# The heads of a graph attention layer: the denominators divided out ahead of Wo, and Wo as 64x64 quarters

## The chip, the cores and the metric

The kernel runs on one core of a Trainium2 chip. A core has five engines that run side by side, each with its own queue in order: TensorE for matrix products (PE in the profile, and PEld for its weight loads), VectorE (DVE), ScalarE (ACT), GpSimd (POOL) and SyncE (SP), which here only issues transfers. 16 DMA engines move data between DRAM and SBUF, the memory on the chip; TensorE writes into PSUM. The metric is the time of one execution on the device in microseconds, as the median of several runs.

## The reference, cut to what matters

Four graph layers run one after the other, each as `x = layernorm(x + layer(x))`, on x of 8 batches, 2048 nodes and 64 features. The change is in the last, a graph attention with 4 heads, followed by a second attention over the product with Wo:

```
h = einsum('bnc,hdc->bhnd', x, Wh)
out_h = gat(h) + bh           # softmax over the neighbours of h.h, times h
cat = out_h as [b, n, 4*64]
z = leaky_relu(cat, 0.2)
h2 = einsum('bnk,dk->bnd', z, Wo)
out2 = gat(h2) + bo
out = layernorm(leaky_relu(out2, 0.2)) * gamma + beta
```

Inside `gat` the sums over the neighbours are divided by the sum of the weights, the denominator, one for each batch, head and node. leaky_relu(a / s) is leaky_relu(a) / s where s is positive, and Wo is linear within a head; so the division may stand at any place from the sums to the sum over heads.

## The kernel before

The graph is sparse. The nodes are handled as 16 tiles of 128 (`NT`), each as 2 groups of 64 nodes (`NG`), each group with 5 sections of 128 gathered neighbours (`GS`): 160 steps for the heads, 10 per tile. A step k consists of these pieces, in a program order that is written out by hand for PE, ACT, DVE and POOL (`manual_schedule`; SP's transfers are issued as the code comes to them):

- `fetch(k + 7)`: POOL gathers 128 rows of 2 KB from the table xtab into xs (L203), 12 buffers
- `turn(k + 2)`: four PE transposes of xs (L1038), copied out by ACT (L1040)
- the work `beside`, one entry for each step of a tile (j = 0 to 9)
- `score(k + 1)`: scores into PSUM (pscore, two buffers, L1051), exponentials on ACT (L1054), times the edges on DVE (L1057)
- `back(k - 1)`: the sums over neighbours on PE (po, L1073). Twice for each group a block of 32 nodes is complete, and DVE copies it to `o` (L1080). xs carries a column of ones, so one row of `o` for each half of the partitions holds the denominators. After the last block of a tile (at j=0 of the next tile) SP writes these two rows to DRAM (dtab, L1084) and reads them back as 32 rows of 128 nodes (dT, L1086).

`beside` before, for the tile ahead (+1) and the tile just summed (-1): j=0 turn_nodes (+1), j=1 sides (+1, heads 0 and 1), j=2 and j=3 through_w (-1), j=4 sides (+1, heads 2 and 3) with `sums` (-1) ahead of it, j=5 to j=8 through_wo (-1, one head each), j=9 pieces (-1).

`through_w` brings two heads of `o` through the weights and leaky_relu into z: its products are `quarters` (L1014), 64x64 blocks of the 128x128 array, then a copy on ACT (L1103) and DVE's leaky product (L1104). z has features on partitions and nodes along the row. `sums` turns dT on PE (L1092) and DVE inverts into recs (L1095, L1097): nodes on partitions. `wo_products` (L1110) multiplies a head's z, four 128x128 blocks, by a block-diagonal Wo into PSUM with nodes on partitions (pm, one buffer); `add_head` multiplies by the inverses on DVE (L1116) and adds the heads up on POOL (L1120). At the last head POOL adds bo (L1124) and SP writes ktab (L1125). `pieces` splits h2 into three bf16 parts on ACT, DVE and POOL (L1138 to L1141), writes them to ptab (L1142), and POOL adds a bias to X (L1143).

The last tile is done after the loop, with add_head on DVE. Then the second attention (`fifth`) gathers from ktab for all tiles. At its end all inverses are checked against bounds (L1383 to L1385); the flag decides whether a slow path runs.

Of the kernel before, what the change touches and what calls it, by code (L numbers as in the profile page):

```python
# [21 lines left out]
F32 = mybir.dt.float32  # L22
# [26 lines left out]
def kernel(ctx: ExitStack, tc: tile.TileContext, ins: dict, out: bass.AP):  # L49
# [622 lines left out]
    f3w = fast.enter_context(tc.tile_pool(name="f3w", bufs=1))  # L672
    recs = f3w.tile([P, NT, HN + 1, B], F32, name="recs")
    early = ExitStack()
# [317 lines left out]
    ktab = dram.tile([N, BD], F32, name="ktab")  # L992
    dtab = dram.tile([NT, 2 * HN * NP, P], F32, name="dtab")
    bo = rows("bo", ins["L3_gnn_bo"], f3w)
    b3 = rows("b3", ins["L3_gnn_beta"], f3w)
    with early, ExitStack() as heads:
# [5 lines left out]
        ps_m = heads.enter_context(tc.tile_pool(name="f3psm", bufs=1, space=PSUM))  # L1002
        Us, os, xss, xsTs, ws, pos, h2s, zs, dTs = ({} for _ in range(9))

# [54 lines left out]
        def back(k):  # L1059
            it, g, s = steps[k]  # L1060
            xs, w = xss.pop(k), ws.pop(k)

            for blk, a, b in blocks_of(s):
                if s == OPEN[blk]:
                    pos[it, g, blk] = ps_o.tile([P, NP, HN, GB], F32, name="po")
                po = pos[it, g, blk]
                for p in range(NP):
                    for k_ in range(2):  # L1070
                        half = slice(k_ * D, (k_ + 1) * D)
                        f0 = p * P + k_ * D
                        nc.tensor.matmul(po[half, p, :, a - blk * GB:b - blk * GB], xs[:, f0:f0 + D],  # L1073
                                         w[:, k_, p, :, a - WINDOWS[s][0]:b - WINDOWS[s][0]],
                                         start=(s == OPEN[blk] and p == 0), stop=(s == CLOSE[blk] and p == NP - 1))
            for blk, a, b in blocks_of(s):
                if s == CLOSE[blk]:
                    if (g, blk) == (0, 0):
                        os[it] = wk.tile([P, HN, NP, P], F32, name="o")
                    nc.vector.tensor_copy(os[it][:, :, :, node_block(g, blk)].rearrange("p h a i -> p a h i"), pos.pop((it, g, blk)))  # L1080
            if (g, s) == (NG - 1, TURN[-1]):
                rows_of = dtab[it].rearrange("(k n) i -> k (n i)", k=2)
                for k_ in range(2):
                    nc.sync.dma_start(rows_of[k_:k_ + 1], os[it][k_ * D:k_ * D + 1].rearrange("p h a i -> p (h a i)"))  # L1084
                dTs[it] = wk.tile([2 * HN * NP, P], F32, name="dT")
                nc.sync.dma_start(dTs[it], dtab[it])  # L1086


        def sums(it, pool=None):
            dT = dTs.pop(it)  # L1090
            pd = pool.tile([P, 2 * HN * NP], F32, name="pt") if pool else misc([P, 2 * HN * NP])
            nc.tensor.transpose(pd, dT, ident[0:2 * HN * NP, 0:2 * HN * NP])  # L1092
            pd = pd.rearrange("p (k h a) -> p h a k", k=2, h=HN)
            rec = recs[:, it, 0:HN].rearrange("p h (a k) -> p h a k", k=2)
            nc.vector.reciprocal(rec[:, :, 0:2], pd[:, :, 0:2])  # L1095
# [3 lines left out]
        def through_w(it, h0):  # L1099
# [4 lines left out]
            nc.vector.scalar_tensor_tensor(z.rearrange(flat), z.rearrange(flat), 0.2, z.rearrange(flat), op0=ALU.mult, op1=ALU.max)  # L1104

        def wo_products(it, h, pool=None):
            z = zs[it, h - h % 2]
# [5 lines left out]
        def add_head(it, h, ph):  # L1113
            eng = nc.vector if it == NT - 1 else nc.gpsimd
            dst = wk.tile([P, B, D], F32, name="h2h" if h else "h2")
            nc.vector.tensor_tensor(dst, ph.rearrange("p a (k d) -> p (a k) d", k=2), along(recs[:, it, h]), ALU.mult)  # L1116
            if h == 0:
                h2s[it] = dst
            else:
                eng.tensor_tensor(h2s[it], h2s[it], dst, ALU.add)  # L1120
            if h == HN - 1:
                h2f = h2s[it].rearrange("p b d -> p (b d)")
                hb = wk.tile([P, B, D], F32, name="hb")
                eng.tensor_tensor(hb, h2s[it], over(bo, hb.shape), ALU.add)  # L1124
                nc.sync.dma_start(ktab[it * P:(it + 1) * P, :], hb.rearrange("p b d -> p (b d)"))  # L1125
                if it == 0:
                    sq = wk.tile([P, BD], F32, name="h2h")
                    nc.scalar.activation(sq, h2f, AF.Square, accum_out=shift)

        def through_wo(it, h):  # L1130
            add_head(it, h, wo_products(it, h))

        def pieces(it):

            h2f = h2s[it].rearrange("p b d -> p (b d)")
            hp3 = wk.tile([P, 3, BD], BF16, name="hp3")
            rest = wk.tile([P, BD], F32, name="rest")
            nc.scalar.copy(hp3[:, 0], h2f)  # L1138
# [6 lines left out]
        def node_side(it, pool, **kw):  # L1145
# [13 lines left out]
        beside = {  # L1159
            0: (turn_nodes, 1), 1: (sides, 1, 0), 2: (through_w, -1, 0), 3: (through_w, -1, 2), 4: (sides, 1, 2),  # L1160
            5: (through_wo, -1, 0), 6: (through_wo, -1, 1), 7: (through_wo, -1, 2), 8: (through_wo, -1, 3), 9: (pieces, -1),
        }
# [4 lines left out]
        with tc.manual_schedule(engines=engines):  # L1167
# [7 lines left out]
            for k in range(len(steps) + 1):  # L1175
# [4 lines left out]
                it, j = divmod(k, PER)  # L1180
                if j == 4 and 0 < it < NT:
                    sums(it - 1)
                f, t, *a = beside[j]
                if k < len(steps) and 0 <= it + t < NT:
                    f(it + t, *a)
                if k + 1 < len(steps):
# [8 lines left out]
            ph = wo_products(t, 0)  # L1195
            sums(t, ps_t)
            add_head(t, 0, ph)
# [4 lines left out]
    with ExitStack() as fifth:  # L1202
# [75 lines left out]
        def invert(it):  # L1278
            nc.vector.reciprocal(recs[:, it, HN], sums[it][1])

        def divide(it):
            po, rd = sums[it][0], recs[:, it, HN]
            z = zs[it] = fk.tile([P, B, D], F32, name="z", bufs=6)
# [95 lines left out]

        nbad = fp.tile([P, 8], F32, name="nbad")  # L1380
        chk = fp.tile([P, NT * (HN + 1) * B], BF16, name="chk")
        recf = recs.rearrange("p t h b -> p (t h b)")
        nc.vector.tensor_scalar(chk, recf, 2.0**-115, None, op0=ALU.is_ge)  # L1383
        nc.vector.scalar_tensor_tensor(chk, recf, 2.0**60, chk, op0=ALU.is_le, op1=ALU.mult, accum_out=nbad[:, 0:1])
        nc.vector.tensor_scalar(nbad[:, 0:1], nbad[:, 0:1], float(NT * (HN + 1) * B), None, op0=ALU.not_equal)  # L1385
        lack = fp.tile([P, 5, NT], F32, name="lack")
# [12 lines left out]
        nc.vector.tensor_scalar(nbad[:, 6:8], bounds[:, 0:2], S_MAX, 1.0, op0=ALU.is_le, op1=ALU.not_equal)  # L1399
        pb = ps_d.tile([1, 8], F32, name="pd")  # L1400
        nc.tensor.matmul(pb, ones_col, nbad, start=True, stop=True)
        sb = fp.tile([1, 1], F32, name="sb")
        nc.vector.tensor_reduce(sb, pb, AX.X, ALU.add)
        nc.vector.tensor_copy(flag, sb)
        bad = nc.values_load(flag[0:1, 0:1], min_val=0, max_val=P * (3 + 5 * NT))
    fast.close()
# [543 lines left out]
```

## Time and profile before

| | us |
|---|---|
| median of 3 runs | 1881.07 (1874.75 to 1881.57) |
| the profiled execution: its time | 1880.07 |
| its span, first to last instruction | 1878.2 |
| PE busy in the span | 1363.0 (73%) |
| DVE busy | 1336.7 (71%) |
| ACT busy | 978.5 (52%) |
| POOL busy | 965.1 (51%) |
| heads stage, first L1038 to the last step | 955 to 1480 |
| L1110, products with Wo: 512 instructions, median of one | 0.275 |
| L1116, DVE, times the inverses: 64, median of one | 0.69 |
| L1120, POOL, sum of the heads: 45 | 1.276 |

The times of the engines overlap, so their sum means nothing; a share of the whole span is an average over stages with different limits, and the one that matters here is that of the heads stage. A product of float32 shows in the profile as two matmul instructions, a transpose as one; the durations of matmuls overlap in the array, so the cost of a group is read from where the next one starts.

### The profile page before, as it was taken

The page shows a single profiled execution, that of the slowest core. Times are in us where ns is not written, and L with a number is a line of the kernel's source. Part 1 is how long each engine was busy: PE and PEld are TensorE (multiplying, and loading weights), DVE is VectorE, ACT ScalarE, POOL GpSimd, SP SyncE. Part 2 cuts the span into 40 slices and gives each one's busy share as a digit, 9 for nine tenths or more (in the row PEclk, how much of TensorE's full clock was granted, in tenths as well). Part 3 has the DMA queues.
Part 4 walks back from the last instruction along what each step waited for, and adds up shares of the span by engine and source line. Part 5 has one row for each costly group of instructions (what it writes and reads, how often), then busy time and mean ns, then how long its engine had stood idle before and what let it go on. Part 6 is the DMA issues. An engine that isn't in the chain of part 4 may idle for free.

```text
span 1878.2 us, 33889 instructions
## 1 busy us (share of the span) xinstructions
PE 1363.0 (73%) x12656; PEld 835.2 (44%) x12656; DVE 1336.7 (71%) x2975; ACT 978.5 (52%) x2405; POOL 965.1 (51%) x889
## 2 busy tenths in 40 slices
PE   3663346551789996997669999999999665566653
PEld 3563223330333334522258888888888521111110
DVE  6879579896676546666735666666666589889887
ACT  4643235545942225355645555555555257677675
POOL 0000376670664543675345565655656388666651
PEclk9955567766799998999779999999999878767776
DMA  7422476660237971365342333332423265455441
GB/s 205 135 90 90 121 203 192 191 202 13 99 113 282 318 265 56 124 194 155 101 118 89 95 110 105 96 119 84 123 87 112 74 191 171 132 154 153 139 111 25
DMA packets 125660, 255.26 MB, mean 136 GB/s; under 512 B 62480, under 2 KB 65040, under 8 KB 123408
## 3 DMA queue, kind: packets, MB, share of 16 engines
q0 software_dynamic: 56320, 188.78, 33.3%
q1 hardware_dynamic: 52528, 60.03, 9.6%
q10 hardware_dynamic: 16640, 4.20, 1.0%
q8 instruction: 102, 1.67, 0.4%
q14 instruction: 70, 0.57, 0.1%
HBM read 217.04 MB, written 35.91 MB: 135 GB/s over the span
## 4 chain that ended last, share of the span: by engine, by line
PE 39%; DVE 12%; ACT 11%; issue 5%; POOL 3%; DMA 1%; ACTq 0%; SPq 0%; POOLq 0%; DVEq 0%
PE pscore L1051 9%; PE po L1073 6%; PE pa L588 5%; PE pt L1038 5%; PE pscore L1014 3%; PE pm L1110 3%; ACT z L169 3%; PE pa L643 2%; ACT wx L1256 2%; DVE sc L1245 2%; PE py L789 2%; DVE pr L1240 1%; DVE st L155 1%; POOL hs L203 1%; PE pa L959 1%
## 5 line engine op out<-in xcount | busy, mean ns | idle before, releaser
L203 POOL DMA_INDIRECT hs<-htab,src x160 | 153.2, 957 | 265.9 <-ACT selTf L431 206.6
L1057 DVE SCALAR_TENSOR_TENSOR w<-w,Sel 128x640 f32<-128x640 f32 (+2 forms) x160 | 170.7, 1073 | 128.2 <-ACT w L1054 128.2
L203 POOL DMA_INDIRECT xs<-xtab,src x160 | 191.6, 1197 | 55.3 <-issue 25.7
L588 PE MATMUL pa<-R,ET 128*128 128x512 bf16 x768 | 182.2, 395 | 49.1 <-POOL R L576 35.7
L203 POOL DMA_INDIRECT hs<-ktab,src x160 | 159.1, 995 | 45.5 <-issue 36.2
L1051 PE MATMUL pscore<-U,xsT 64*128 64x80 f32 (+2 forms) x2560 | 182.1, 282 | 0.0
L1051 PEld LDWEIGHTS pscore<-U,xsT 64*128 64x128 f32 x2560 | 156.9, 189 | 37.2 <-ACT xsT L1040 22.7
L1054 ACT ACTIVATE w<-pscore 128x640 f32<-128x640 f32 (+2 forms) x160 | 119.6, 748 | 99.9 <-PE pscore L1051 98.8
L169 ACT ACTIVATE X<-X,ln_m,ln_r 128x64 f32<-128x64 f32 x256 | 87.2, 428 | 138.9 <-DVE ln_m L161 138.9
L588 PEld LDWEIGHTS <-ET 128*128 128x128 fp8e4 x768 | 75.4, 101 | 163.8 <-issue 85.4
L1040 ACT COPY xsT<-pt 128x512 f32<-128x512 f32 x160 | 93.7, 586 | 100.5 <-PE pt L1038 99.5
L1235 PE MATMUL pe<-hi,selTb 64*128 64x512 bf16 x480 | 89.0, 489 | 74.7 <-DVE pr L1240 69.0
L1120 POOL TENSOR_TENSOR h<-h,h2h 128x512 f32<-128x512 f32 x45 | 57.4, 1276 | 161.7 <-DVE h2h L1116 161.7
L1073 PE MATMUL po<-w,xs 128*64 128x88 f32 (+2 forms) x3072 | 138.7, 236 | 1.1 <-DVE w L1057 1.1
L1038 PE MATMUL pt<-ident,xs 128*128 128x128 f32 x640 | 106.3, 289 | 25.0 <-DMA xs<-xtab,src 23.9
L1073 PEld LDWEIGHTS po<-w,xs 128*64 128x64 f32 x3072 | 113.4, 137 | 15.0 <-DVE w L1057 1.4
L203 POOL DMA_INDIRECT rs<-rtab,src x80 | 75.9, 949 | 62.4 <-PE pa L643 43.0
L1240 DVE TENSOR_TENSOR pr<-pe,hs 128x1024 f32<-128x1024 f32 x80 | 97.3, 1216 | 14.6 <-DMA hs<-ktab,src 10.7
L1256 ACT ACTIVATE wx<-hs,w 128x64 f32<-128x64 f32 x424 | 106.7, 344 | 0.0
L597 DVE RECIPROCAL rec<-pa 128x256 f32<-128x256 f32 x32 | 54.1, 1730 | 64.1 <-PE pa L643 38.0
L1245 DVE TENSOR_REDUCE sc<-pr 128x16 f32<-128x1024 f32 x80 | 97.1, 1214 | 2.0
L460 DVE TENSOR_TENSOR hs<-hs,w 128x1024 f32<-128x1024 f32 x80 | 91.8, 1212 | 3.2 <-ACT w L449 3.2
(628 smaller groups left out, 3188.4 us busy)
## 6 DMA issues: line engine op xcount, KB each, us to landing
at<-in_adj SPq DMA_DIRECT2D x16, 1024.0 KB
rtab<-r SPq DMA_DIRECT2D x16, 512.0 KB
ptab<-hp SPq DMA_DIRECT2D x16, 384.0 KB
hi<-ptab SPq DMA_DIRECT2D x16, 384.0 KB
X<-in_x ACTq DMA_DIRECT2D x16, 256.0 KB
htab<-H SPq DMA_DIRECT2D x16, 256.0 KB
ytab<-y SPq DMA_DIRECT2D x16, 256.0 KB
ktab<-hb SPq DMA_DIRECT2D x16, 256.0 KB
```

The source lines that it names most:

```text
L169: nc.scalar.activation(v[:, b], v[:, b], AF.Identity, scale=rstd[:, k:k + 1], bias=nmr[:, k:k + 1])
L203: nc.gpsimd.indirect_dma_start(out=dst, out_offset=None, in_=table[:, :], in_offset=bass.IndirectOffsetOnAxis(ap=src[:, it, s, g:g + 1], a ...
L588: nc.tensor.matmul(po[h].rearrange("p a f -> p (a f)"), ET[:, jt, it * P:(it + 1) * P], R[:, jt, q, h].rearrange("p a f -> p (a f)"), star ...
L1038: nc.tensor.transpose(pt[:, p], xss[k][:, p * P:(p + 1) * P], ident)
L1040: nc.scalar.copy(xsTs[k], pt)
L1051: nc.tensor.matmul(pscore[:, k_, f0:f0 + HN * ni].rearrange("p (h i) -> p h i", i=ni), xsT[half, p], Us[it][half, p, :, i0:i0 + ni], start ...
L1054: nc.scalar.activation(w.rearrange("p k a h i -> p k (a h i)"), pscore[:, :, 0:NP * HN * ni], AF.Exp)
L1057: nc.vector.scalar_tensor_tensor(wt, wt, 3.0e38, edge, op0=ALU.min, op1=ALU.mult)
L1073: nc.tensor.matmul(po[half, p, :, a - blk * GB:b - blk * GB], xs[:, f0:f0 + D], w[:, k_, p, :, a - WINDOWS[s][0]:b - WINDOWS[s][0]], start ...
L1240: nc.vector.tensor_tensor(pr.rearrange("p k b d -> p (k b d)"), pes[u].rearrange("p k b d -> p (k b d)"), hss[u].rearrange("p k b d -> p ( ...
L1245: nc.vector.tensor_reduce(sc, pr, AX.X, ALU.add)
L1256: nc.scalar.activation(wxs[u][:, 0, b], hss[u][:, 0, b], AF.Copy, scale=ws[u][:, 0, b:b + 1])
```

## The change

The division moves from behind Wo to ahead of it. In place of `sums` (at j=4) there is `invert` at j=3: DVE inverts dT as it lies (32 rows of 128), SP writes the inverses to a DRAM table itab and reads them back as R, broadcast over the 64 partitions of each half: four transfers with 64 x 4 runs of 256 numbers, 1 MB together. DVE also checks the bounds of the inverses here, on the 32 rows. At j=5 and j=6 `divide` multiplies z by R on POOL, two heads at a time. At j=7 `wo_all` multiplies all four heads by Wo as 64x64 quarters with 256 columns and adds the heads up in PSUM (in a pscore buffer); ACT copies the sum out as hT, features on partitions. At j=8 `turn_back` transposes hT, four times 128x128, ACT and DVE copy the result to h2, with the two halves of the partitions put back in their places, and POOL adds bo as before. DVE's products with the inverses and POOL's additions of the heads are gone, but for the last tile, which keeps the old way with `last_invert`. `o`, `h2h` and `rest` have one buffer in place of two. The checks at the end take the inverses of the second attention, those of the last tile, and the counts from `invert`.

```diff
-    recs = f3w.tile([P, NT, HN + 1, B], F32, name="recs")
+    recs = f3w.tile([P, NT, B], F32, name="recs")
+    last_recs = f3w.tile([P, HN, B], F32, name="last_recs")
+    RD = 2 * HN * NP
+    recT = f3w.tile([RD, P], F32, name="recT")
+    few = f3w.tile([RD, NT], F32, name="few")
...
-                        os[it] = wk.tile([P, HN, NP, P], F32, name="o")
+                        os[it] = wk.tile([P, HN, NP, P], F32, name="o", bufs=1)
...
-        def sums(it, pool=None):
+        def invert(it):
             dT = dTs.pop(it)
...
+            rT = wk.tile([RD, P], F32, name="rT")
+            nc.vector.reciprocal(rT, dT)
+            nc.sync.dma_start(itab[it], rT)
+            nc.vector.tensor_scalar(recT, rT, 2.0**-115, None, op0=ALU.is_ge)
+            nc.vector.scalar_tensor_tensor(recT, rT, 2.0**60, recT, op0=ALU.is_le, op1=ALU.mult, accum_out=few[:, it:it + 1])
+            R = Rs[it] = wk.tile([P, HN, 2, 2, P], F32, name="R", bufs=1)
+            rows_of = itab[it].rearrange("(k h j a) i -> k h j (a i)", k=2, h=HN, j=2)
+            for q in range(2):
+                for j in range(2):
+                    nc.sync.dma_start(R[q * D:(q + 1) * D, :, j].rearrange("p h a i -> p h (a i)"),
+                                      rows_of[q if j == 0 else 1 - q, :, j].unsqueeze(0).to_broadcast([D, HN, 2 * P]))
...
+        def divide(it, h0):
+            z = zs[it, h0].rearrange("p j h a n -> p j h (a n)")
+            nc.gpsimd.tensor_tensor(z, z, Rs[it][:, h0:h0 + 2].rearrange("p h j a n -> p j h (a n)"), ALU.mult)
+
+        def wo_all(it):
+            ph = ps_s.tile([P, 2, CW], F32, name="pscore")
+            for h in range(HN):
+                z = zs[it, h - h % 2]
+                for k in range(2):
+                    own = slice(k * D, (k + 1) * D)
+                    for j in range(2):
+                        to = own if j == 0 else slice((1 - k) * D, (2 - k) * D)
+                        nc.tensor.matmul(ph[to, j, 0:2 * P], WoT[own, h, own],
+                                         z[own, j, h % 2].rearrange("p a n -> p (a n)"), start=(h == 0), stop=(h == HN - 1))
+            hTs[it] = wk.tile([P, 2, 2, P], F32, name="hT")
+            nc.scalar.copy(hTs[it].rearrange("p j a n -> p j (a n)"), ph[:, :, 0:2 * P])
+
+        def turn_back(it):
+            hT = hTs.pop(it)
+            ph = misc([P, 2, 2, 2, D])
+            for j in range(2):
+                for a in range(2):
+                    nc.tensor.transpose(ph[:, j, a].rearrange("p k d -> p (k d)"), hT[:, j, a], ident)
+            h2s[it] = wk.tile([P, B, D], F32, name="h2")
+            h2 = h2s[it].rearrange("p (j a k) d -> p j a k d", j=2, a=2)
+            nc.scalar.copy(h2[:, 0], ph[:, 0])
+            for k in range(2):
+                nc.vector.tensor_copy(h2[:, 1, :, k], ph[:, 1, :, 1 - k])
+            with_bo(it, nc.gpsimd)
...
-            0: (turn_nodes, 1), 1: (sides, 1, 0), 2: (through_w, -1, 0), 3: (through_w, -1, 2), 4: (sides, 1, 2),
-            5: (through_wo, -1, 0), 6: (through_wo, -1, 1), 7: (through_wo, -1, 2), 8: (through_wo, -1, 3), 9: (pieces, -1),
+            0: [(turn_nodes, 1)], 1: [(sides, 1, 0)], 2: [(through_w, -1, 0)], 3: [(invert, -1), (through_w, -1, 2)],
+            4: [(sides, 1, 2)], 5: [(divide, -1, 0)], 6: [(divide, -1, 2)], 7: [(wo_all, -1)], 8: [(turn_back, -1)], 9: [(pieces, -1)],
...
-                if j == 4 and 0 < it < NT:
-                    sums(it - 1)
```

## The prediction

> **What bounds the kernel now.** I read the busy time by stage first, then the waits inside the stage that the change touches, then one tile of that stage in order of time. The heads stage runs from 955 us (first turn of a gathered tile, L1038) to 1480 us. Three rows of the table of stretches; the columns are the length, then busy time of PE, PEld, DVE, ACT, POOL, the granted clock, the DMA share and GB/s:
>
> ```profile
> 1100.00:1200.00 100.00, 100.00 (x1506) 83.31 (x1506) 64.49 (x83) 54.63 (x83) 59.62 (x48) 1.00 0.35 105
> 1200.00:1300.00 100.00, 100.00 (x1513) 83.87 (x1512) 63.76 (x83) 54.94 (x83) 59.63 (x48) 1.00 0.34 102
> 1300.00:1400.00 100.00, 100.00 (x1505) 83.92 (x1503) 63.77 (x80) 54.43 (x82) 59.65 (x48) 1.00 0.34 101
> ```
>
> PE is busy all the time at a granted clock of 1.00; DVE has a third of its time free, POOL 40%. In the waits from 1100 to 1400 us the longest is POOL's at L1120, which costs nothing; PE's queue has none over 0.4 us. So a microsecond of PE work added or removed moves the end, and so does any wait put into PE's order. The period of a tile is 32.70 us (its o copies end at 1190.48 and 1223.18). Now one tile in order of time (start, length):
>
> ```profile
> 1190.50 0.53 SPq L1084 DMA_DIRECT2D dtab<-o  x2
> 1190.72 0.66 PE L1038 MATMUL pt<-ident,xs 128*128 128x128 f32 x4
> 1191.30 0.64 PEld L1014 LDWEIGHTS pscore<-o,AT 64*64 64x64 f32 x16 [0.17 <-DVE U L1024]
> 1192.33 0.97 PEld L1051 LDWEIGHTS pscore<-U,xsT 64*128 64x128 f32 x16 [0.39 <-ACT xsT L1040]
> 1193.73 0.31 SPq L1086 DMA_DIRECT2D dT<-dtab  x1
> ...
> 1195.87 0.96 POOL L203 DMA_INDIRECT xs<-xtab,src  x1 [0.30 <-issue]
> ...
> 1201.41 0.65 PE L1038 MATMUL pt<-ident,xs 128*128 128x128 f32 x4
> 1201.80 0.97 PEld L1110 LDWEIGHTS pm<-WoT,z 128*128 128x128 f32 x8
> 1202.89 0.97 PEld L1051 LDWEIGHTS pscore<-U,xsT 64*128 64x128 f32 x16
> ...
> 1207.16 1.28 POOL L1120 TENSOR_TENSOR h<-h,h2h 128x512 f32<-128x512 f32 x1 [9.07 <-DVE h2h L1116]
> ...
> 1215.44 0.97 PEld L1051 LDWEIGHTS pscore<-U,xsT 64*128 64x128 f32 x16 [0.17 <-issue]
> ...
> 1217.20 0.66 PE L1038 MATMUL pt<-ident,xs 128*128 128x128 f32 x4
> 1217.58 0.47 PEld L699 LDWEIGHTS pm<-ident,X 128*128 128x128 f32 x4
> ...
> 1218.22 0.97 PEld L1051 LDWEIGHTS pscore<-U,xsT 64*128 64x128 f32 x16 [0.17 <-issue]
> ```
>
> The reader is to see the gap that a piece of work makes between a step's turn (pt) and its score. With one head through Wo it is 1202.89 - 1201.41 = 1.48 us; with nothing between 0.59 (in the ninth step pt starts at 1214.85, score at 1215.44); with four 128x128 transposes 1.03 (1217.19 to 1218.22); one call of quarters, eight 64x64 products of two heads, takes 1.03 (1191.30 to 1192.33) after 0.59 of approach.
>
> **The change on PE.** I write j for the step in the tile. j=4 loses the transpose of the denominators (1198.46 to 1198.63): -0.17. j=5 and j=6 lose a head each: 1.48 to 0.59, -0.89 twice. j=7 gets wo_all, sixteen 64x64 products of 256 columns, which is two calls of quarters: 0.59 + 2 x 1.03 = 2.65 for 1.48, +1.17. j=8 gets turn_back, four transposes: 1.03 for 1.48, -0.45. Sum -1.23 us per tile. The last tile keeps the old way, so 15 tiles: -18.5 us, if PE never waits.
>
> **The new chain.** Now the denominators are needed before Wo, and they get there by o copy, dtab, dT, reciprocal, itab, R, two divisions on POOL. Before, the inverses were first used at j=5 through a path that ended at j=4 on PE. I count from T, the end of the last o copy, when dtab is issued (1190.50).
>
> - dtab to dT landed. dT is issued 3.2 us after dtab here, 2.5 (1288.60 to 1291.07) to 4.2 (1027.11 to 1031.34) in others; at the last tile, where PE waits for it, dT lands 1.63 after its issue (1481.75 to 1483.38). While gathers run it is later: the packets of dT end between 4.5 and 7.0 us after T, median 5.2, plus 0.2 for the semaphore. T+5.4. DVE is free by T+5.0 (its score product of j=2 ends at 1195.47), so it stands waiting; behind it stands through_w's second leaky product, wanted only at j=7.
> - Reciprocal of 32x128. L1095 takes 244 ns for 16 columns, L597 1730 for 256: 6.2 ns a column, 0.93 us. T+6.3.
> - itab written, R issued. The pair dtab, dT gives 2.2 to 3.9 from the last write's issue to the read's issue; 2.75. T+9.1. SP has nothing else queued until ktab at j=8.
> - R: four DMAs, 64x4 rows of 1 KB each, 1 MB per tile. The trace has 128 packets of 1 KB for xtab at 929.4 to 930.1 us at about 300 GB/s: 3.5 us, after 0.9 us from issue to first packet (ktab at 1184.53 starts to move at 1185.4) and before 0.3 of completion. T+13.8. Bounds: 2.5 us at the 420 GB/s of ktab's best slices, 7.0 if the rate halves because each DMA writes 64 partitions and not 128. The nearer row has packets of the same size, so 3.5.
> - divide, 128x1024 on POOL, twice, with the gather of j=6 between them. An addition of two 128x512 takes 1276 ns; a cast goes from 724 (512) to 1323 (1024), so 125 ns are fixed and 1024 columns cost 2.4. Bounds: 1.91 (L1261, where one operand is repeated) and 2.55. Gather 1.25 and 0.3 of issue. L1057 on DVE grows from 0.82 to 2.67 us at most when POOL adds or multiplies at the same time, so the two hold each other up; I give the second divide 0.3. T + 13.8 + 2.4 + 1.55 + 0.3 + 2.4 + 0.1 = T+20.6.
>
> **Where PE needs it.** Without waits pt of j=7 would come at 1207.96 - 1.95 = 1206.01; the heads 2 and 3 of wo_all then start 0.59 + 1.03 later, at 1207.63, T+17.1. The first division is ready at T+16.2, just in time for heads 0 and 1. So PE waits 3.5 us at wo_all in each tile. Queued behind it on PE are the score and the sums of that step, on ACT the copy hT and the exponentials, so the stall goes through to T of the next tile and isn't made up. Net 3.5 - 1.23 = +2.3 us per tile, 15 tiles: +34.5 us.
>
> [...]
>
> **What lies beside.** DVE loses four products of 0.69 and three small reciprocals per tile and gets the 0.93, two checks of 32x128 (0.2 each at most, from 128x8 at 0.17 and 128x640 at 0.49) and two copies of 128x128 (0.2 to 0.3): lighter by over 1 us. POOL loses three additions (3.8 us) and gets 4.8: 24 us of a 35 us period. While it waits for R, about 7 us, no gather is issued; seven steps of gathers are ahead, over 16 us, which hides it; without that cover the 7 us would fall on PE. ACT gets hT (0.59, as L1040) and half of h2 (0.35), in gaps of 45% of its time. The score product blocked by a division (2.4) has 4 us until its sums (exponentials of 1204 feed sums at 1210). o with one buffer is next written at j=3, when its products and dtab are 3 us past. The checks at the end replace 1.44 us of DVE (L1383 to L1385) by some ten operations of 0.1 to 0.25 us in a place where DVE waits for ACT until 1861.7: nothing, 0.5 us if ACT were early. The last tile's tail from 1480 us, on the old path, is the same.
>
> **Sum.** Span 1878.2 + 34.5 = 1912.7, with the 1.9 us around it (1880.07) 1914.6; the median of the runs shown, 1881.07, lies 1.0 above the profiled time, so 1915.
>
> **Rivals.**
> 1. The chain fits. With every low bound, dT at T+4.1, reciprocal 0.9, itab 2.2, R 0.9 + 2.5 + 0.2, divisions of 1.91 and a gather of 1.25, the second division ends at T+16.0, before PE asks at T+17.1. Then the full 18.5 us are won: 1862.5. It needs my chain to be 3.5 us too long; at 2.3 too long the change is level. For it: POOL idles there and SP has nothing else to do. Against: five steps in a row at the low end. Chance 0.14, with 0.11 between this and level, near 1881.
> 2. R is the long pole: its rate halved, 7.0 us, stall 7.0, net +5.8 per tile, +87: 1968; at the midpoint of the two times +60, 1941. For it: halves of 64 partitions and one source read by 64 rows. Against: the 1 KB row. It decides from R over 5 us. Chance 0.18.
> 3. wo_all isn't two calls of quarters, because four heads add up in the same PSUM rows and each has to wait for the one ahead: twice the time, 2.06 more, of which the first half hides under the stall; +15 us on the forecast, 1930, or 1881 to 1893 if the chain fits. For it nothing in this trace; L1073 adds in PSUM without a gap. Chance 0.05.
>
> **How the numbers follow.** The forecast as it stands, 1893 to 1940, has 0.52; it is the likeliest, so 1915. With rivals 2 and 3 slower has 0.75, within 0.5% (about what a measurement of this kernel can tell from no change, 9 us) 0.11, faster 0.14. The range goes down to 1869, which takes in level and part of the gain, and up to 1955, R at about 6.2 us; the likeliest case alone is 1893 to 1940.
>
> **What will show it.** PE's idle time before the wo_all line, released by POOL's division, near 3.5 us times 15, and PE's busy share in the stage falling to about 90%; a period of 35 us; dT to R landed about 8.4 us; divisions of 2.4 us with POOL idle before the first, ended by DMA R; wo_all's products in 2.1 us. The prediction is wrong if POOL reaches the first division after R has landed, if the waits of PE name another engine, or if the tile is shorter than 32.7 us.

## The result and the profile after

The changed kernel takes 2002.21 us (median of 6 runs, 1999.36 to 2005.74); the kernel before takes 1880.51 beside it (6 runs, 1874.75 to 1881.57). The ratio is 1.065, 95% interval 1.063 to 1.067: 122 us slower, where 34 were forecast and the range reached to 74. The direction was right, the size was not. A single run more than 1.5% above the fastest of its kernel (there are two, both on a slower chip of the experiments) is left out of the times and ratios below.

First the table of stretches of the changed kernel, with the columns and the stretches that the prediction showed of before:

```profile
1100.00:1200.00 100.00, 89.57 (x1228) 71.00 (x1226) 44.42 (x61) 47.05 (x74) 48.85 (x37) 0.85 0.37 105
1200.00:1300.00 100.00, 86.87 (x1236) 67.89 (x1232) 46.92 (x64) 46.84 (x71) 46.67 (x37) 0.88 0.41 113
1300.00:1400.00 100.00, 89.23 (x1180) 70.24 (x1184) 41.44 (x58) 45.16 (x71) 49.01 (x37) 0.81 0.37 105
```

PE is idle for 11.4% of the time (265.66 of 300 busy), and, what no term of the prediction allowed for, its granted clock is 0.81 to 0.88 where it was 1.00. In the same busy time fewer products get done: 1180 to 1236 per 100 us, before 1505 to 1513. The writes to dtab come at 1197.31, 1238.11 and 1279.42: a tile takes 40.8 to 41.3 us in place of 32.70, 8.1 to 8.6 more, and 15 tiles by 8.1 are the 122 us.

Now one tile in order of time (start, length, engine, line, shape; in brackets the idle time of the engine just before, and what ended it):

```profile
1197.31 0.53 SPq L1089 DMA_DIRECT2D dtab<-o  x2
...
1200.33 0.31 SPq L1091 DMA_DIRECT2D dT<-dtab  x1
...
1202.93 0.94 DVE L1097 RECIPROCAL rT<-dT 32x128 f32<-32x128 f32 x1
...
1203.90 0.31 SPq L1098 DMA_DIRECT2D itab<-rT  x1
...
1206.58 2.92 SPq L1105 DMA_DIRECT2D R<-itab  x4
...
1211.60 1.13 PE L1056 MATMUL pscore<-U,xsT 64*128 64x88 f32 x16
...
1214.41 2.34 POOL L1127 TENSOR_TENSOR z<-z,R 128x1024 f32<-128x1024 f32 x1 [10.18 <-DMA R<-itab]
...
1216.81 1.09 PE L1137 MATMUL pscore<-z,WoT 64*64 64x256 f32 x16 [2.79 <-POOL z L1127]
1217.92 2.35 POOL L1127 TENSOR_TENSOR z<-z,R 128x1024 f32<-128x1024 f32 x1
...
1220.32 1.99 PE L1137 MATMUL pscore<-z,WoT 64*64 64x256 f32 x16 [2.41 <-POOL z L1127]
...
1222.23 2.00 PE L1056 MATMUL pscore<-U,xsT 64*128 64x80 f32 x16
```

Two things are to be seen. PE waits twice per tile, here 2.79 and 2.41 us, 5.20 together, each time for a division. And after the second wait the same work takes almost twice as long: the second half of wo_all 1.99 for 1.09 of the first, the score's sixteen products 2.00 for 1.13 before the wait. The stretches of 3 us through this place show why:

```profile
1211.00:1214.00 3.00, 3.00 (x43) 2.42 (x40) 2.00 (x3) 1.52 (x3) 0.00 (x0) 1.00 0.63 136
1214.00:1217.00 3.00, 0.21 (x5) 0.19 (x8) 0.46 (x1) 0.58 (x1) 2.44 (x2) 1.00 0.00 0
1217.00:1220.00 3.00, 0.90 (x16) 0.32 (x10) 0.00 (x0) 0.00 (x0) 2.98 (x2) 0.82 0.32 87
1220.00:1223.00 3.00, 2.69 (x24) 1.57 (x24) 0.00 (x0) 0.59 (x1) 2.21 (x3) 0.50 0.23 64
1223.00:1226.00 3.00, 3.00 (x44) 2.80 (x42) 0.83 (x1) 0.70 (x1) 0.00 (x0) 0.50 0.38 116
1226.00:1229.00 3.00, 3.00 (x20) 2.64 (x20) 0.49 (x2) 0.96 (x2) 0.00 (x0) 0.50 0.00 0
1229.00:1232.00 3.00, 3.00 (x48) 2.56 (x46) 1.53 (x2) 1.70 (x3) 2.23 (x2) 0.97 0.23 87
```

The last three columns are the granted clock, the DMA share and GB/s. The clock falls to half within the second wait (0.82 over 3 us is 1.08 us at 0.50, so from about 1218.9) and comes back at about 1229.2: 10.2 us at half speed in this tile, for 8.8 of which PE is busy. So the account of this tile, 40.80 us long, has three terms: -1.2 of PE work saved, +5.2 of waits, and the +4.1 that remain of the 8.1, near what 8.8 us of work lose at half the clock. That the third term is real, and a term of its own, is what the experiments had to show.

In other tiles the clock falls earlier. Here are three stretches of the tile above and two of a later one, cut at multiples of 3.41 us: in this trace every change of the clock comes a multiple of that after the one before (1.00 from 1188.19 to 1218.91, 0.50 to 1229.15, 1.00 to 1256.46).

```profile
1212.08:1215.49 3.41, 1.94 (x32) 1.52 (x30) 1.59 (x3) 1.61 (x3) 1.07 (x1) 1.00 0.22 42
1215.49:1218.91 3.42, 1.09 (x16) 0.51 (x16) 0.00 (x0) 0.00 (x0) 3.25 (x3) 1.00 0.14 20
1218.91:1222.32 3.41, 2.00 (x18) 0.89 (x18) 0.00 (x0) 0.00 (x0) 2.95 (x3) 0.50 0.20 67
...
1334.97:1338.38 3.41, 1.81 (x30) 1.40 (x28) 1.46 (x2) 1.49 (x3) 1.38 (x1) 1.00 0.23 42
1338.38:1341.79 3.41, 1.99 (x16) 0.80 (x16) 0.00 (x0) 0.00 (x0) 3.24 (x3) 0.50 0.14 23
```

In the heads stage of the two traces of the changed kernel (this one and that of the next section) each of the 30 falls comes at the end of such a stretch in which PE was busy for 1.82 us or less, and none at the end of one with 1.86 or more. So one wait is enough: in eight of the 15 tiles here the clock falls within the first, in seven of these only 1.6 to 2.0 us after PE stopped. Then the first half of wo_all takes 1.99 us, and the second wait is shorter by as much (1.5 for 2.4). Over the 15 tiles the two waits are 3.8 to 5.6 us together, 4.7 on average, and the half speed lasts 10.2 to 17.1 us, 12.5 on average.

### The profile page after: what moved, and what is told of

Read it like the earlier page. It is cut to its first block, busy times and chain, and to the rows that moved or that the text cites. A ratio compares the mean times of both kernels' runs of the same rounds, so it can differ in the third digit from the quotient of the medians.

```text
span 2001.9 us, 34012 instructions
## 1 busy us (share of the span) xinstructions
PE 1408.8 (70%) x12701; PEld 848.4 (42%) x12701; DVE 1305.7 (65%) x2967; ACT 993.0 (50%) x2435; POOL 966.2 (48%) x874
## 4 chain that ended last, share of the span: by engine, by line
PE 23%; DVE 14%; ACT 12%; DMA 10%; issue 6%; POOL 6%; SPq 2%; POOLq 0%; ACTq 0%; DVEq 0%
PE pa L588 5%; PE pscore L1056 4%; DMA R<-itab 4%; PE po L1078 3%; ACT z L169 2%; POOL z L1127 2%; PE pa L643 2%; PE pt L1043 2%; ACT wx L1301 2%; DMA itab<-rT 2%; PE py L793 2%; DVE sc L1290 2%; DMA dT<-dtab 2%; SPq L1105 2%; PE pscore L1137 1%
## 5 line engine op out<-in xcount | busy, mean ns | idle before, releaser
L1062 DVE SCALAR_TENSOR_TENSOR w<-w,Sel 128x640 f32<-128x640 f32 (+2 forms) x160 | 158.8, 993 | 281.5 <-ACT w L1059 281.3
L1056 PE MATMUL pscore<-U,xsT 64*128 64x80 f32 (+2 forms) x2560 | 204.8, 306 | 0.0
L203 POOL DMA_INDIRECT xs<-xtab,src x160 | 178.3, 1114 | 53.4 <-issue 29.0
L1056 PEld LDWEIGHTS pscore<-U,xsT 64*128 64x128 f32 x2560 | 178.5, 212 | 51.6 <-issue 28.5
L1078 PE MATMUL po<-w,xs 128*64 128x88 f32 (+2 forms) x3072 | 152.5, 251 | 0.0
L1127 POOL TENSOR_TENSOR z<-z,R 128x1024 f32<-128x1024 f32 x30 | 71.7, 2390 | 156.7 <-DMA R<-itab 135.8
L1078 PEld LDWEIGHTS po<-w,xs 128*64 128x64 f32 x3072 | 126.7, 152 | 14.7 <-issue 0.3
L1043 PE MATMUL pt<-ident,xs 128*128 128x128 f32 x640 | 113.2, 303 | 24.5 <-DMA xs<-xtab,src 23.8
L1137 PE MATMUL pscore<-z,WoT 64*64 64x256 f32 x480 | 54.1, 593 | 69.9 <-POOL z L1127 69.9
```

The lines of the kernel that those rows point to most:

```text
L203: nc.gpsimd.indirect_dma_start(out=dst, out_offset=None, in_=table[:, :], in_offset=bass.IndirectOffsetOnAxis(ap=src[:, it, s, g:g + 1], a ...
L1043: nc.tensor.transpose(pt[:, p], xss[k][:, p * P:(p + 1) * P], ident)
L1056: nc.tensor.matmul(pscore[:, k_, f0:f0 + HN * ni].rearrange("p (h i) -> p h i", i=ni), xsT[half, p], Us[it][half, p, :, i0:i0 + ni], start ...
L1062: nc.vector.scalar_tensor_tensor(wt, wt, 3.0e38, edge, op0=ALU.min, op1=ALU.mult)
L1127: nc.gpsimd.tensor_tensor(z, z, Rs[it][:, h0:h0 + 2].rearrange("p h j a n -> p j h (a n)"), ALU.mult)
```

## The experiments

The runs fell on several chips. On the first and on the one of the next section the kernel before takes 1880 us; on five others it takes 1969 to 1989. So ratios are given only against runs of the kernel before on the same chip. Why those chips are slower is told where the kernel before was profiled on one of them.

### The clock alone: products that nobody reads, in the waits

Theory A: the loss has two parts, the waits and the clock that falls after them. The rival has only one cause, the late division, and a slow clock as its harmless trace. The edit fills PE's waits ahead of each half of wo_all with products into a PSUM buffer that is not read:

```diff
+        def warm(n):
+            pw = misc([P, HN, P])
+            for _ in range(n):
+                nc.tensor.matmul(pw.rearrange("p h n -> p (h n)"), ident, WoT.rearrange("p h n -> p (h n)"), start=True, stop=True)
...
+                if h % 2 == 0:
+                    warm(2 if h else 3)
```

> Edit: PE gets products that nothing uses (identity times WoT, 512 columns), three ahead of wo_all's heads 0 and 1 and two ahead of heads 2 and 3, so that PE is busy while it waits for the divisions. Nothing else changes, and the chain to R keeps its length. Theory A, the fall of the granted clock to 0.50 after the wait is a cost of its own (in the changed kernel the score after wo_all takes 2.00 us where 1.12 is usual, about 4.1 us per tile): clock near 1.00 in the heads stage, time 2002 - 15 x 4.1 = 1940. Theory B, those products are slow for another reason (the four heads added up in PSUM, traffic of R): time stays at 2002, score after wo_all at 2.0 us.

Measured on a chip where before takes 1988.83: 2050.18, ratio 1.031 (1.029 to 1.034). The changed kernel without the edit did not run on that chip, where PE has stops of its own, so this run alone settled nothing. The same kernel ran again, with both kernels unchanged beside it.

> The kernel before, once more, with a profile on the chip of these runs. On the chip of the first experiments it took 1989 us and not 1880, and PE sat idle with nothing to wait for that the profile shows (issue). If chips differ so, the profile shows this idle time on PE here too; on a chip like the first 1880 and no such idle time in the heads stage.

> The changed kernel, once more, beside the same runs. On a chip like the first: 2002, 8.1 us per tile over the kernel before, of which 5.2 us waits at wo_all and 4.1 us slow products after them, less 1.2 saved. On a chip that stalls on issue, the difference to the kernel before is smaller, since stalls ahead of the waits hide in them.

> The products that nothing uses, once more (three ahead of wo_all's heads 0 and 1, two ahead of heads 2 and 3). Theory A, the fall of the clock is a cost of its own: clock near 1.00 in the heads stage, and 60 us less than the changed kernel in the same call (1940 for 2002). Theory B, no cost of its own: the same time as the changed kernel.

Here all three ran on one chip, and this chip behaves like the first. Before 1879.94 (ratio 0.999, 0.998 to 1.000, against the other runs of the same kernel); changed 2003.50 (1.066, 1.063 to 1.068); with the products in the waits 1942.41 (1.032, 1.031 to 1.034). A stretch of the changed kernel on this chip:

```profile
1100.00:1200.00 100.00, 88.49 (x1212) 70.12 (x1214) 43.35 (x60) 46.24 (x73) 49.37 (x37) 0.85 0.37 104
```

The same stretch with the products in the waits, and from its timeline the place of wo_all (here L1144; the idle products are L1132):

```profile
1100.00:1200.00 100.00, 98.13 (x1364) 71.38 (x1362) 52.14 (x69) 51.04 (x78) 55.80 (x41) 1.00 0.43 123
```

```profile
1156.43 0.66 PE L1043 MATMUL pt<-ident,xs 128*128 128x128 f32 x4
1156.92 2.74 PE L1132 MATMUL pm<-WoT,ident 128*128 128x512 f32 x6
1159.78 1.09 PE L1144 MATMUL pscore<-z,WoT 64*64 64x256 f32 x16
1160.81 1.98 PE L1132 MATMUL pm<-WoT,ident 128*128 128x512 f32 x4
1163.30 1.09 PE L1144 MATMUL pscore<-z,WoT 64*64 64x256 f32 x16 [0.51 <-POOL z L1127]
1164.32 1.12 PE L1056 MATMUL pscore<-U,xsT 64*128 64x80 f32 x16
```

The clock stands at 1.00, and the products behind the waits have their old lengths: 1.09 in both halves, 1.12 in the score. The waits themselves are all still there, only filled: from pt to score are 7.89 us (1164.32 - 1156.43). Doing nothing useful, but without a pause, wins 61 us (2003.50 - 1942.41), which is 4.1 per tile: the clock's part of the loss. The other 62 us over before, 4.2 per tile, are the waits less the PE work saved (5.2 - 1.2 = 4.0; a tile of this kernel takes 36.69 us, 3.99 more than before). Theory A holds.

### R by itself

R, from its issue to the division that uses it, takes 7.8 us in the tile above, where the prediction put 4.7. The probe adds transfers of the same size at the end of the kernel, beside the gathers of the second attention: into 64 partitions in four pieces, or into 128 in two; broadcast from itab, or each partition its own rows of xtab.

```diff
+                        if n < 2:
+                            src_ = one[q, :, j].unsqueeze(0).to_broadcast([np_, HN, 2 * P])
+                        else:
+                            r0 = (q * D + j * P) * HN
+                            src_ = xtab[r0:r0 + np_ * HN, 0:2 * P].rearrange("(p h) c -> p h c", h=HN)
+                        nc.sync.dma_start(dst, src_)
```

> Edit: after the last store SP runs, twice each and one after the other, 1 MB loads in four forms: four DMAs of 64 partitions from one broadcast source (as R), two of 128 partitions broadcast, four of 64 partitions from rows of their own, two of 128 partitions from rows of their own. The outputs are the same, the time isn't compared. R in the changed kernel: 5.9 us from first to last packet, 7.8 from issue to use. Theory P, writing 64 partitions has half the rate: forms 1 and 3 near 5.9 us, forms 2 and 4 near 3.3. Theory S, reading the same rows is slow: forms 1 and 2 near 5.9, forms 3 and 4 near 3.3. Theory I, the issue of a DMA with 256 runs (0.61 to 0.73 us each) sets the pace: with half as many DMAs of twice the runs the issue stays at 2.4 us or more in total and all forms take the same.

SP's issues in the timeline of this kernel, one of each kind:

```profile
1717.85 2.58 SPq L1438 DMA_DIRECT2D probe<-itab  x4
...
1731.52 0.92 SPq L1438 DMA_DIRECT2D probe<-itab  x2
...
1742.52 2.49 SPq L1438 DMA_DIRECT2D probe<-xtab  x4
...
1753.95 1.21 SPq L1438 DMA_DIRECT2D probe<-xtab  x2
```

The packets of 1 KB, from the trace's records of the DMA engines, took 74 to 78 ns into 64 partitions (four readings, broadcast or not) and 46 to 50 ns into 128. So it is neither the broadcast nor the table: with half the partitions each packet took 1.5 to 1.7 times as long. And four transfers cost SP 2.5 us to issue, where two of the same bytes cost 0.9 to 1.2. The times of the whole transfers, 4.5 to 9.2 us from first packet to last, are blurred by the gathers beside them and decide nothing.

A second run changes R inside the changed kernel: two transfers with runs of 8 KB. For this the rows of dtab have to be written in another order, in four pieces.

```diff
-                                      rows_of[q if j == 0 else 1 - q, :, j].unsqueeze(0).to_broadcast([D, HN, 2 * P]))
+            for q in range(2):
+                nc.sync.dma_start(R[q * D:(q + 1) * D].rearrange("p h j a i -> p (h j a i)"),
+                                  itab[it].rearrange("(k n) i -> k (n i)", k=2)[q:q + 1].to_broadcast([D, 8 * 2 * P]))
```

> The changed kernel with R read in two transfers of 64 partitions by 8 KB in place of four of 64 by 4 runs of 1 KB; for that dtab is written in four pieces and not two, so that the rows stand in the order in which they are read. The bytes and the partitions stay. Theory A (R's size makes the waits, and the fall of the clock only follows from them): fewer and longer runs are issued in about 1 us in place of 2.7, so R is there 1.5 to 2.5 us earlier, less 0.5 for the two more writes; the waits of PE on POOL's divisions fall from 5.2 to 3 or 4 us per tile. If the clock still falls, 1975 to 1990 on a chip where before takes 1880; if it stays at 1.00, near 1920. Theory B (the packets into 64 partitions, and not the number of runs, set R's length): R takes as long as before, waits 5.2 to 5.7, 2000 to 2010.

2048.05 where before takes 1988.33: 1.034 (1.029 to 1.038). SP in one tile:

```profile
1197.76 2.46 SPq L1096 DMA_DIRECT2D dtab<-o  x4
1202.36 0.33 SPq L1098 DMA_DIRECT2D dT<-dtab  x1
1208.24 0.31 SPq L1105 DMA_DIRECT2D itab<-rT  x1
1209.66 1.14 SPq L1110 DMA_DIRECT2D R<-itab  x2
```

By the time alone this run says nothing, since the changed kernel did not run on that chip, and the four pieces of dtab took 2.46 us of SP in place of 0.53, which put dT off. But R can be read. Its issue fell from 2.92 to 1.14 us, and from issue to its last packet it takes 6.3 us (1209.66 to 1215.92), in the changed kernel 7.2 (1206.58 to 1213.81). Its 128 packets of 8 KB took 579 ns each, 72 ns for 1 KB; the 1024 packets of the changed kernel 67 ns each in the tile above, 61 to 81 over all tiles. So the runs' length does not matter here, as theory B said, and neither does the number of transfers, which in the probe had changed together with the partitions: two transfers into 64 partitions still take 64 to 74 ns for 1 KB over all tiles. Fewer issues are worth 0.9 us in the tiles shown and 0.5 on average (6.8 and 6.3 us from issue to last packet), and most of R's length lies in the packets into 64 partitions.

### wo_all later

If the waits are the root of both losses, giving the chain more steps of cover must win both back. Four kernels move wo_all (and what follows it) to later steps of the tile. First by one step:

```diff
-            0: [(turn_nodes, 1)], 1: [(sides, 1, 0)], 2: [(through_w, -1, 0)], 3: [(invert, -1), (through_w, -1, 2)],
-            4: [(sides, 1, 2)], 5: [(divide, -1, 0)], 6: [(divide, -1, 2)], 7: [(wo_all, -1)], 8: [(turn_back, -1)], 9: [(pieces, -1)],
+            0: [(pieces, -2), (turn_nodes, 1)], 1: [(sides, 1, 0)], 2: [(through_w, -1, 0)], 3: [(invert, -1), (through_w, -1, 2)],
+            4: [(sides, 1, 2)], 5: [(divide, -1, 0)], 6: [(divide, -1, 2)], 7: [], 8: [(wo_all, -1)], 9: [(turn_back, -1)],
```

> Edit: wo_all one step later (j=8), turn_back at j=9, pieces at j=0 of the next tile. PE's need comes one step of 2.36 us later. Theory A: of the 5.2 us of PE's waits at wo_all 2.9 are left, each wait under 3 us; if the clock then stays at 1.00 the period is 32.7 - 1.2 + 2.9 = 34.4 and the time about 1906; if it still falls to 0.50, about 1965. Rival, the cost lies in wo_all or the divisions themselves and not in where they stand: 2002.

> The variant with wo_all one step later (j=8), once more, on the chip of this call; on the chip of the first call PE stood still on issue. Theory A: each wait at wo_all under 3 us, so the clock stays at 1.00 in most tiles; period 34.4, 1906. If the clock still falls after waits of 0.4 and 2.4 us: about 1965.

1998.26 where before takes 1988.83 (1.005, 1.003 to 1.008), and on a second chip 2005.19 beside 1987.86 (1.008, 1.006 to 1.010). The time that was expected, 1906, is a ratio of 1.014 to the 1880 that it was worked out from; the two don't compare closely, since PE stops by itself on such chips in the kernel before too, and on one of them the whole change costs a ratio of 1.047 (last experiment). But against that too most of the loss is gone with one step of 2.4 us. It takes away one wait of the two: mostly one is left, 2.2 us on average in the first run (17.6 us in 8) and 2.6 in the second (23.1 in 9). The clock does not stay at 1.00, as theory A had it for waits under 3 us: from 1100 to 1300 us it stands at 0.93 to 0.97 in the first run and at 0.90 in the second, and no run shows such a limit: in the changed kernel the clock fell at 1338.38 within a wait of 2.69.

By two steps, with turn_back and pieces at j=0 and j=1 of the tile after:

```diff
+            0: [(turn_back, -2), (turn_nodes, 1)], 1: [(sides, 1, 0), (pieces, -2)], 2: [(through_w, -1, 0)], 3: [(invert, -1), (through_w, -1, 2)],
+            4: [(sides, 1, 2)], 5: [(divide, -1, 0)], 6: [(divide, -1, 2)], 7: [], 8: [], 9: [(wo_all, -1)],
```

> Edit: wo_all two steps later (j=9), turn_back at j=0 and pieces at j=1 of the next tile, the last pieces after the loop. Theory A: waits at wo_all of 0.5 us or less, clock 1.00, period 31.5 to 32.0, time 1862 to 1872, faster than the kernel before: the 1.23 us saved on PE are real. Rival 1: PE saves nothing by the quarters, time 1881. Rival 2: POOL and DVE, in each other's way, become late and PE waits for the edge products: over 1890.

A miss: 2041.09, ratio 1.027 (1.024 to 1.030), where one under 1 was expected, and although wo_all has more cover than in the run before. SP's timeline:

```profile
1185.10 0.52 SPq L1089 DMA_DIRECT2D dtab<-o  x2
1190.59 0.34 SPq L1189 DMA_DIRECT2D ptab<-hp  x1
1191.04 0.36 SPq L1091 DMA_DIRECT2D dT<-dtab  x1
```

ptab, which pieces writes, now stands in SP's queue between dtab and dT. It waits for POOL until 1190.59, and dT behind it leaves 5.9 us after dtab in place of 3.0 (4.2 to 6.2 in 13 of the 15 tiles). The chain starts one to three microseconds later, so PE's waits for the divisions are still there, two in each tile (28.8 us in 14 from 1100 to 1400 us); another 8.5 us in 7 are for the PSUM buffer that turn_back and turn_nodes share. With pieces at j=4 instead:

```diff
+            0: [(turn_back, -2), (turn_nodes, 1)], 1: [(sides, 1, 0)], 2: [(through_w, -1, 0)], 3: [(invert, -1), (through_w, -1, 2)],
+            4: [(sides, 1, 2), (pieces, -2)], 5: [(divide, -1, 0)], 6: [(divide, -1, 2)], 7: [], 8: [], 9: [(wo_all, -1)],
```

> Edit: wo_all at j=9, turn_back at j=0 of the next tile, pieces at j=4 of the next tile, so that on SP's queue ptab stands behind R and no more ahead of dT (where it held dT back by 2.9 us in the variant with pieces at j=1). Theory A: waits at wo_all under 0.5 us, clock 1.00, 1862 to 1872 where the kernel before takes 1880, that is 10 to 18 us below it in the same call. Rival: PE saves nothing by the quarters, the same as before or above.

On the chip of the clock's run: 1895.17 beside 1879.94, ratio 1.007 (1.006 to 1.009), so again not the gain that was expected. The clock is 1.00, the period 33.43, and PE's timeline has two idle times left in a tile:

```profile
1190.79 0.63 PE L703 MATMUL pm<-ident,X 128*128 128x128 f32 x4 [1.18 <-DVE h L1152]
...
1219.16 1.09 PE L1137 MATMUL pscore<-z,WoT 64*64 64x256 f32 x16 [0.55 <-POOL z L1127]
```

turn_back and turn_nodes in one step share a PSUM buffer, and pieces' work on POOL stands ahead of the division. Without these two, 33.43 - 1.18 - 0.55 = 31.70 would be a tile's time, 1.0 below the 32.70 of before. One more wait stands at the end of the stage: the pieces of the last tile but one come behind the loop, their ptab leaves ahead of the last dT, and PE waits 5.1 us for it, before 0.8. The last kernel gives each its own step (with turn_nodes of the second tile ahead of the loop, and the pieces of the last tile but one behind it):

```diff
+            0: [(turn_back, -2)], 1: [(sides, 1, 0)], 2: [(through_w, -1, 0)], 3: [(invert, -1), (through_w, -1, 2)],
+            4: [(sides, 1, 2)], 5: [(divide, -1, 0)], 6: [(divide, -1, 2)], 7: [(pieces, -2)], 8: [(turn_nodes, 2)], 9: [(wo_all, -1)],
```

> Edit on the variant with wo_all at j=9 (1895 us): pieces go behind the divisions (j=7 of the next tile), so that POOL is free when R lands (there it began the first division 1.2 us after, behind the bias addition to X), and turn_nodes goes from j=0 to j=8, two tiles ahead, so that it does not wait for the PSUM buffer of turn_back (1.18 us of PE per tile there); the last pieces after the loop, turn_nodes(1) ahead of it. Theory: the waits of PE were all that kept the saving from showing, 33.4 - 1.2 - 0.6 = 31.6 us per tile, 1865 to 1870, 10 to 15 below the kernel before. Rival: the saving on PE isn't real; 1880 or above although PE waits for nothing.

> The kernel of the run e8_late4 once more, for the size of what it wins, if possible on a chip where the kernel before takes 1880. Theory A (the PE work saved is real, 1.23 us by 15 tiles, once nothing waits for the divisions): 18.5 us faster than before, 1861 to 1866 where before takes 1880, 1968 where it takes 1988; PE's waits on POOL in the heads stage none, its granted clock 1.00. Rival (the order with turn_back and pieces two tiles late costs what the quarters save, and the win on the other chip was its slower instruction supply): within 5 us of before.

> The changed kernel with the products with Wo at j=9, turning back and splitting two tiles late. Theory A (the PE work saved, 1.23 us by 15 tiles, is won once nothing waits for the divisions): 1861 to 1866 where before takes 1880, period of a tile 31.5; 1965 to 1975 where before takes 1988. Rival (the win came from the instruction supply alone): within 5 us of before where that takes 1880.

> The same kernel as f_late4. Theory A (1.23 us of PE work saved in each of 15 tiles): where before takes 1880, 1861 to 1866, the period of a tile 31.5 us, PE 100% busy at a clock of 1.00 in the heads stage. Rival (turning back and splitting later cost what the quarters save): 1875 to 1885, period 32.5 to 33.

It ran on four chips, none of them one where before takes 1880:

| | us | before there | ratio (95%) |
|---|---|---|---|
| first | 1968.66 | 1987.86 | 0.991 (0.989 to 0.993) |
| second | 1973.34 | 1988.33 | 0.993 (0.991 to 0.995) |
| third | 1963.70 | 1971.74 | 0.994 (0.991 to 0.998) |
| fourth | 1954.35 | 1968.97 | 0.993 (0.990 to 0.996) |

Faster than the kernel before on each, by 8 to 19 us: under 1%, but each interval lies below 1. The 18.5 of the sum were reached once; on all four PE still waits 5.1 us for the last dT, which takes some 4 of them. The changed kernel ran on the third of these chips alone (2061.97, next section). The fourth run's timeline of PE through wo_all and turn_back (L1147):

```profile
1156.29 0.66 PE L1043 MATMUL pt<-ident,xs 128*128 128x128 f32 x4
1156.87 2.05 PE L1137 MATMUL pscore<-z,WoT 64*64 64x256 f32 x32
1158.85 1.12 PE L1056 MATMUL pscore<-U,xsT 64*128 64x80 f32 x16
...
1160.60 0.66 PE L1043 MATMUL pt<-ident,xs 128*128 128x128 f32 x4
1161.10 0.60 PE L1147 MATMUL pm<-ident,hT 128*128 128x128 f32 x4
1161.63 1.14 PE L1056 MATMUL pscore<-U,xsT 64*128 64x96 f32 x16
```

With nothing to wait for, wo_all makes a gap of 2.56 us (1158.85 - 1156.29) and turn_back one of 1.03. These are near the prediction's 2.65 and 1.03, so the PE work that the change saves is real, and on these chips an order exists that keeps most of it. How much a chip with no stops of its own would show, and with it the rival that the win needs these stops, is open: on none of the four does the kernel before take 1880.

### Both kernels on a slower chip

> The kernel before with a profile, on the chip of the two runs beside it. Where it takes 1880: PE busy 100 us in each 100 us of the heads stage, clock 1.00. Where it takes 1988: theory A, PE and its weight loads wait on issue in each 100 us of the heads stage and elsewhere, with the clock at 1.00 or a little under; theory B, all waits as on the first chip and the clock lower throughout.

> The changed kernel on the same chip. Theory A (waits of 4.1 us net and 4.1 us of slow clock per tile): where before takes 1880, 2000 to 2006; where it takes 1988, the stops of the supply lie partly within the waits, and 2050 to 2110, with a clock of 0.80 to 0.92 in the heads stage. Rival (on a chip whose supply stops PE the waits are covered): within 20 us of before.

Before 1970.45 (ratio 0.9995, 0.997 to 1.002), changed 2061.97, ratio 1.047 (1.042 to 1.053): the change loses 90 us there too, so the rival, that stops of PE's own would cover the waits, falls. The kernel before, its stretch and PE's longest wait of the heads stage (us in total, times, longest):

```profile
1100.00:1200.00 100.00, 94.69 (x1313) 77.75 (x1312) 55.66 (x71) 47.36 (x71) 51.52 (x41) 0.95 0.29 86
```

```profile
PE po L1073 <- issue: 15.3, 36, 1.1
```

On this chip PE stops again and again on "issue", with no engine and no transfer in the profile to wait for (15.3 us from 1100 to 1400); on the chip of the clock's run PE's queue has no wait at all in this stretch. The period of a tile is 36.7 in place of 32.70. What delays PE's instructions there was not tried; that it is their supply, as the expectations have it, no run shows.

## Why the prediction was wrong

- **The PE work saved, -1.23 us per tile: right.** wo_all measured 2.56 for 2.65, turn_back 1.03 for 1.03, and at j=5 and j=6 of the changed kernel the score follows pt by 0.59 (1211.01 to 1211.60 in the tile shown). Rival 3, that adding four heads in the same PSUM rows is slow, falls with the 2.05 us of all 32 products.
- **The chain up to R: right.** From T, the issue of dtab: reciprocal at +5.6 (forecast 5.4), itab at +6.6 (6.3), R issued at +9.3 (9.1).
- **R: wrong size, 7.8 us for 4.7.** I had chosen the row of xtab's 1 KB packets, 3.5 us, as "the nearer row", with 7.0 as the other bound. That row has packets of the right length, but it is into DRAM from 128 partitions, and the probe shows that 1 KB takes 46 to 50 ns with 128 partitions and 74 to 78 with 64; the number of partitions was what mattered, not the length of the run. That 64 partitions halve the rate, as the other bound and rival 2 have it, no run shows: the probe's packets took 1.5 to 1.7 times as long. In the tile shown the packets went on for 5.9 us (1207.94 to 1213.81; 4.9 to 6.0 over the tiles), after 1.4 to the first for 0.9, with 0.6 to the division for 0.3. Rival 2 pointed this way, its condition (over 5 us) was met, and I gave it 0.18.
- **The divisions: right.** 2.34 and 2.35 for 2.4, the second 3.5 after the first for 4.25. Together with R the stall is 5.2 us for 3.5.
- **The step that failed: "Net 3.5 - 1.23 = +2.3 us per tile".** It prices a wait at its own length and the work behind it as before. The work behind it ran at half the clock for 10.2 us in the tile shown (12.5 on average), 4.1 us more, which is half of the loss and was in no term, no rival and no bound. I had read the granted clock of 1.00 in three rows as a property of the stage; PE's queue had no wait over 0.4 us there, and in the changed kernel on the chip of the clock's run the stage was at 0.85 with its waits empty and at 1.00 with them filled (1100 to 1200 us). The prediction did not ask what its 3.5 us of stall would do to the clock. The trace shows it: the clock changes at multiples of 3.41 us, and in the stretch ahead of the fall (1215.49 to 1218.91) PE still worked for 1.09 us, in others for up to 1.82.
- **The sum.** Forecast -1.23 + 3.5, by 15 tiles: +34.5. Measured, in the terms of the tile shown, -1.2 + 5.2 + 4.1, by 15: +122. With R's true size alone it would have been -1.2 + 5.2, by 15: +60, and the run in which the clock was kept up measured 62 over before.
- **Terms off without effect.** POOL's "24 us" of a period leave out the 3.8 that it loses: 60% of 32.7 is 19.5, with -3.8 and +4.8 it is 20.5. The two checks on DVE take 0.38 and 0.35 us for 0.2.
- **What should have shown it.** The idle time in front of wo_all, released by POOL, is there with 5.2 us; PE's busy share is 88.6% near the 90% named. That agreement is misleading, since a busy PE at half the clock counts as busy (3.00 us of 3 at 0.50 from 1223 to 1226). The period of 35 us, now 40.9, is the sign that failed. And the table of stretches of before has rows, behind the heads stage, with PE busy for 39% and 63% and the clock at 0.66 and 0.76:

```profile
1480.00:1520.00 40.00, 15.71 (x88) 7.39 (x90) 24.19 (x35) 10.01 (x31) 21.97 (x23) 0.66 0.50 156
1520.00:1700.00 180.00, 114.23 (x685) 34.02 (x684) 163.00 (x275) 126.11 (x481) 126.24 (x111) 0.76 0.54 155
```

## What to carry to other kernels

The waits put into a TensorE queue that had none cost their length, 5.2 us in the tile shown, and then, for the time that the clock stayed down, 4.1 more. In the changed kernel an idle time of 1.6 to 2 us within a stretch of 3.41 was enough. Where such a wait can't be avoided, an estimate from this trace is half speed for the work in the 10 to 17 us behind it; or fill the wait with products that nobody reads, which won 61 us here. Give a new chain through DRAM its cover in steps first, and look at each queue it passes: one transfer that waited in SP's queue ahead of another (ptab ahead of dT, which then left 5.9 us after dtab in place of 3.0) took back the cover that was given. And price a transfer from a row with the same number of partitions: here 1 KB took 74 to 78 ns into 64 of them and 46 to 50 into 128.

## What was not expected of the hardware

- In the heads stage of the changed kernel the granted clock went by the busy time of PE in stretches of 3.41 us: it fell after each with 1.82 us or less and after none with 1.86 or more, though no wait had to fill a stretch. In the variant with pieces at j=4, with waits of 1.18 and 0.55 us, which stand in different places of the tile, it stayed at 1.00. But busy time as the profile counts it isn't all. In the kernel before, outside the heads stage, one stretch with 1.55 us (1816.75 to 1820.16) brought no fall and one with 2.46 (232.98 to 236.40) brought one. On the slower chip of the last experiment the clock of the kernel before was 0.95 from 1100 to 1200 us, with PE busy for 94.69 of them and no wait of PE over 1.1 us.
- Once down, it was at 0.50 for 10.2 us in the tile shown, though PE was busy without a pause for the last 8.8 of them (1220.32 to 1229.15). In 29 of the 30 falls in the heads stage of the two traces, two or three stretches with PE busy throughout had to pass; in the kernel before, behind that stage, nine of 25 falls lasted for one stretch alone (as from 1533.45 to 1536.86, with PE busy for 3.41 us).
- 1 KB packets into 64 partitions took 74 to 78 ns, into 128 partitions 46 to 50; packets of 8 KB into 64 partitions 508 to 594 (means of a tile), about the same rate.
- The same kernel takes 1880 us on some chips and 1969 to 1989 on others, where PE's queue stops on "issue" (15.3 us of 300 where it was profiled); the difference is about as large as the whole loss, so a comparison across chips would say nothing.
